# Moving the written-block and position passes, and the unseen-position mask, behind the first quarter of layer 1

## The chip, the cores and the metric

The kernel runs on one core of one Trainium2 chip. The metric is device time in microseconds (us), the median over several executions; lower is better. The core has engines that each work through their own queue in order: TensorE (PE, matrix products), VectorE (DVE), ScalarE (ACT), GpSimd (POOL), and SyncE (SP), which here only issues DMAs. They meet through semaphores: an instruction that waits holds up everything behind it in its own queue.

## The reference, cut to what matters

Two layers over 1024 tokens (32 sequences of 32, width 256), all in fp32. Layer 0: a gathered 32x32 mix per sequence, a LayerNorm attention, a LoRA feed-forward and a gated feed-forward. Layer 1: a causal attention (`L1_cond`), a linear attention over memory banks (`L1_attn`), a paged attention (`L1_cond2`), and a mixture of 16 experts (`L1_ffn`). The part that the change touches prepares the paged attention:

```python
pos = kv_lens[:, None] + jnp.arange(Tx)          # 32 new positions of each sequence
q, k = _rope(q, pos), _rope(k, pos)              # cos and sin of pos
blk = jnp.take_along_axis(block_tables, pos // BLOCK, axis=1)
k_blocks = k_blocks.at[blk, :, pos % BLOCK, :].set(k.transpose(0, 2, 1, 3))
v_blocks = v_blocks.at[blk, :, pos % BLOCK, :].set(v.transpose(0, 2, 1, 3))
k_all, v_all = (c[block_tables] for c in (k_blocks, v_blocks))
# attention over the last WINDOW = 128 keys at or before each position
```

Sequences may share blocks, so a key that a sequence reads can have been written by another one. The kernel therefore works out, for every slot of every block that is read, which new token wrote it last, or none. That is the search for the written blocks. Its result is a row number for every key, kept in `at`.

## The kernel before, in words

The 1024 tokens are worked in four quarters (`NQ = 4`) of 256. Layer 0's attention runs for quarters 0 to 3 (`mha`, L346, called in the loop at L464); `feed_forward(0)` (L558) follows; then come the preparations of the paged attention; then, in the loop at L903, `layer1(q)` and `feed_forward(q + 1)` for q = 0 to 3. The paged attention and the experts come last.

The order on each engine is not written out. The tile scheduler plays the program through with its own costs and, each time an engine comes free, takes of the instructions that are ready the one that was emitted first. So a part that is emitted later fills the gaps of the parts before it, and `feed_forward(q + 1)` fills those of `layer1(q)` on TensorE. `behind(first, *later)` (L178) adds an edge of order alone: on their engine, `later` come after `first`. `attended` is the last addition of layer 0's attention (L483); `weighted` is the list of the last softmax passes of each `mha` half (L403).

The steps that matter here, in their order of emission before the change:

- **The block rows** (L561 to L587, in pool `ix`): four rounds. POOL gathers the key and value blocks into `raw` (two tiles, tags a0 and a1 of `apool`), copies them into row order `rr` (two buffers), and SP stores each `rr` to `rows_d`.
- **The written blocks and the positions' rows** (L595 to L682): passes over `sw`, `fs`, `wb`, `eq`, then four rounds of `t`, `ok`, `most`, `last` (L610 to L633), and four of `ec`, `mt` (L647, L648) with `ovl`, all on DVE. SP stores `last` to `win_d`; POOL gathers `wsel` from it (L654), makes `newi`; SP stores it to `at_d`; POOL gathers `run` (L678) and casts it to `runf` (L682).
- **The rotation tables** (L685 to L718): `pos`, `ang`, `kf`, `r` on DVE, two Sin activations on ACT (L711), and eight products into `turn`.
- **The mask of unseen positions** (L727 to L744): pool `bad` loads a constant, POOL makes `low` and `bad` for 32 sequences, and fills `none`, which SP spreads over the experts' table `xs_d`. The profile shows its first POOL pass waiting for the last store of `rr`.
- **`layer1(q)`** (L765): `mha` makes scores from `QT` (L767), `KT`, `vblk` (L369) and `kb` (L378); then come the memory banks (L810 to L841), `x3T` (L845), and rotated keys and queries (L876). `x3T` and `qall` take the tags a0 and a1, thus the places of `raw`. In quarter 1, TensorE transposes `runf` into `at` (L849, L851). `at` is first read by the gathers of the paged attention (L945), and `bad` by its scores (L987).

## Time and profile before

| what | value |
|---|---|
| time, median of 3 runs | 712.08 us (706.6 to 713.12) |
| the profiled execution | 711.48 us |
| its span, first to last instruction | 709.2 us |
| mean granted TensorE clock | 0.914 of full speed |
| PE, DVE, ACT, POOL busy in the span | 83%, 53%, 26%, 27% |

The profiled execution lasts 711.48 us, of which 2.3 us lie outside the span. Its time is 0.6 us under the median. Times within the span are counted from its first instruction. In timeline rows the columns are the start, the duration, the engine, the line of the program, the operation, what it writes and reads, and how many such instructions were merged; in brackets stands how long the engine was idle before it and what ended that. Passes of one engine overlap by some 0.07 us, so that a row's duration is a little longer than the step to the next row.

### The profile page before, as it was taken

To read this page: it belongs to the slowest core of one execution; us is meant where nothing else is said; L and a number is where in the kernel's file an instruction comes from. 1 tells how busy PE (TensorE), PEld (TensorE's weight loads), DVE (VectorE), ACT (ScalarE), POOL (GpSimd) and SP (SyncE) were. 2 spreads that over 40 slices of the span, in tenths; PEclk is the share of its full clock that TensorE was granted. 3 is DMA by queue.
4 is the path that set the end of the run, shared out by engine and by line. 5 is a ranking of instruction groups with operands and counts; after the bars stand their busy time and mean duration, and the time that the engine had idled before them with its cause. 6 is when DMAs were issued, how large, how long until landed. Compare 5 with 4: busy or idle time off the path is not lost.

```text
span 709.2 us, 9084 instructions
## 1 busy us (share of the span) xinstructions
PE 585.9 (83%) x3246; PEld 452.0 (64%) x3246; DVE 377.3 (53%) x872; ACT 187.5 (26%) x492; POOL 192.2 (27%) x280
## 2 busy tenths in 40 slices
PE   3679999995999999999999986655888998079990
PEld 2457877872888867888678864443666665056660
DVE  4748476799544284423754244332577737035553
ACT  1313232322212031311313221022566623012220
POOL 4013003345569700000000000007664101724450
PEclk9959999997999999999999995685899999679996
DMA  6945003454363000000000063003221000224315
GB/s 167 380 154 66 18 1 121 132 150 108 100 201 96 0 1 1 16 0 1 1 1 15 1 257 142 1 26 105 85 71 49 1 1 15 104 66 125 115 48 178
DMA packets 37452, 55.35 MB, mean 78 GB/s; under 512 B 8906, under 2 KB 29536, under 8 KB 36576
## 3 DMA queue, kind: packets, MB, share of 16 engines
q1 hardware_dynamic: 27549, 37.62, 16.3%
q0 software_dynamic: 5904, 15.40, 8.1%
q10 hardware_dynamic: 3955, 1.75, 0.9%
q8 instruction: 26, 0.43, 0.3%
q14 instruction: 18, 0.15, 0.1%
HBM read 38.56 MB, written 18.17 MB: 80 GB/s over the span
## 4 chain that ended last, share of the span: by engine, by line
PE 59%; DVE 16%; issue 8%; POOL 7%; DMA 4%; ACT 4%; POOLq 0%; SPq 0%; DVEq 0%; ACTq 0%
PE ff L188 27%; PE mm L188 13%; POOL ys_d L1271 4%; DVE kb L378 3%; PE tr L412 3%; PE mm L835 3%; DVE vblk L369 2%; PE po L1011 2%; ACT sm L993 2%; PE tr L406 1%; PE sc L979 1%; PE sc L385 1%; POOL xs_d L1201 1%; DVE sm L987 1%; PE mm L1196 1%
## 5 line engine op out<-in xcount | busy, mean ns | idle before, releaser
L945 POOL DMA_INDIRECT kv<-rows_d,at x40 | 38.8, 970 | 245.2 <-DMA sh_g<-in_L_ffn_sWg 234.7
L583 POOL COPY rr<-raw 88x256 f32<-88x256 f32 x64 | 29.3, 489 | 89.0 <-PE tr L459 47.4
L524 DVE SCALAR_TENSOR_TENSOR th<-th,ff 128x512 f32<-128x512 f32 x32 | 21.7, 679 | 51.0 <-ACT th L523 50.9
L378 DVE TENSOR_TENSOR kb<-KT,con 128x1024 f32<-128x1024 f32 x32 | 38.3, 1218 | 9.2 <-ACT KT L473 5.6
L1271 POOL DMA_INDIRECT ys_d<-yb,xb x31 | 30.5, 985 | 44.9 <-DVE yb L1269 44.6
L385 PE MATMUL sc<-kb,QT 128*32 128x256 f32 x256 | 22.4, 424 | 20.1 <-DVE kb L378 15.8
L1256 PE MATMUL gu<-ew,xT 128*128 x124 | 34.4, 400 | 3.2 <-issue 2.5
L523 ACT ACTIVATE th<-ff 128x512 f32<-128x512 f32 x32 | 19.1, 597 | 64.8 <-PE ff L188 56.1
L188 PE MATMUL ff<-x,w_g 128*128 128x256 f32 x128 | 35.5, 392 | 0.0
L188 PE MATMUL ff<-x,w_u 128*128 128x256 f32 x128 | 34.3, 381 | 0.0
L188 PE MATMUL ff<-y,f_w_gate 128*128 128x256 f32 x128 | 31.5, 381 | 0.0
L188 PE MATMUL ff<-y,f_w_up 128*128 128x256 f32 x128 | 31.0, 380 | 0.0
L1250 PE MATMUL xt<-ident,xb 128*128 128x128 f32 x62 | 11.8, 291 | 21.7 <-DMA xb<-xs_d 21.6
L188 PE MATMUL ff<-h,d_Wd 128*128 128x256 f32 x128 | 29.8, 381 | 0.0
L188 PE MATMUL ff<-h,f_w_down 128*128 128x256 f32 x128 | 28.3, 379 | 0.0
L1256 PEld LDWEIGHTS gu<-ew,xT 128*128 128x128 f32 x124 | 23.1, 199 | 7.7 <-issue 2.8
L993 ACT ACTIVATE sm<-sm,mx 128x160 f32<-128x160 f32 x64 | 26.7, 418 | 4.6 <-DVE mx L991 3.6
L525 DVE SCALAR_TENSOR_TENSOR h<-th,ff 128x512 f32<-128x512 f32 x32 | 21.9, 684 | 10.7 <-PE ff L188 10.1
L188 PEld LDWEIGHTS ff<-x,w_g 128*128 128x128 f32 x128 | 23.9, 194 | 4.7 <-issue 1.6
L188 PEld LDWEIGHTS ff<-x,w_u 128*128 128x128 f32 x128 | 24.1, 190 | 4.0 <-issue 0.8
L979 PE MATMUL sc<-KT,qz 128*128 128x160 f32 x128 | 25.3, 335 | 1.7 <-DVE qz L965 1.3
L385 PEld LDWEIGHTS sc<-kb,QT 128*32 128x32 f32 x256 | 5.3, 111 | 33.3 <-DVE kb L378 22.4
(337 smaller groups left out, 1342.1 us busy)
## 6 DMA issues: line engine op xcount, KB each, us to landing
ew<-in_L_ffn_W SPq DMA_DIRECT2D x1, 6144.0 KB
rows_d<-rr SPq DMA_DIRECT2D x32, 176.0 KB
xs_d<-none SPq DMA_DIRECT2D x1, 3999.0 KB
xb<-xs_d SPq DMA_DIRECT2D x31, 129.0 KB
x<-in_x SPq DMA_DIRECT2D x4, 256.0 KB
w_u<-in_L_cond_Wu SPq DMA_DIRECT2D x1, 1024.0 KB
w_g<-in_L_cond_Wg SPq DMA_DIRECT2D x1, 1024.0 KB
d_Wd<-in_L_cond_Wd SPq DMA_DIRECT2D x1, 1024.0 KB
```

Source lines behind the costliest of these rows:

```text
L188: mm_ = te.matmul(ps, lhsT=a, rhs=b, start=j == 0, stop=j == len(pairs) - 1)
L378: v.tensor_tensor(kb, KT[:, m, js].rearrange("p (b k) -> p b k", b=4).unsqueeze(2).broadcast_to([P, 4, 8, 32]), m8.unsqueeze(1).unsqueeze( ...
L385: te.matmul(ps[32 * b4 : 32 * b4 + 32, m * 256 : (m + 1) * 256], lhsT=QT[:, m, j * P + 32 * b4 : j * P + 32 * b4 + 32], rhs=kb[:, b4].rear ...
L412: te.matmul(av[64 * (hg % 2) : 64 * (hg % 2) + 64, hg // 2, 32 * b4 : 32 * b4 + 32], lhsT=vblk[:, j, b4, hg, :], rhs=PT[:, hg, 32 * b4 : 3 ...
L524: v.scalar_tensor_tensor(flat(t), flat(t), 1.0, flat(pg), ALU.add, ALU.mult)
L525: v.scalar_tensor_tensor(flat(h[:, f : f + 2]), flat(t), 0.5, flat(pu), ALU.mult, ALU.mult)
L583: g_.tensor_copy(r[:, :, j].rearrange("p o g d -> p g o d"), raw[j].rearrange("p (g a o d) -> a p g o d", g=4, a=8, d=32)[a],)
L945: got = g_.indirect_dma_start(out=kv[:, a, :], out_offset=None, in_=rows_d, in_offset=bass.IndirectOffsetOnAxis(ap=at[:, g, a : a + 1], ax ...
L979: te.matmul(ps[:, h, :], lhsT=q.qz[:, b, h].rearrange("p g t -> p (g t)"), rhs=q.KT[:, b, :], start=True, stop=True,)
L993: s.activation(sm[:, h], sm[:, h], AF.Exp, bias=mx[:, h : h + 1], accum_out=q.su[:, b, h : h + 1])
L1256: te.matmul(pg[:, :D], lhsT=xT[:, k * P : (k + 1) * P], rhs=w[:, k * D : (k + 1) * D], start=k == 0, stop=k == 1)
L1271: g_.indirect_dma_start(out=ys_d, out_offset=bass.IndirectOffsetOnAxis(ap=xb[:, D + 1 :].bitcast(I32), axis=0), in_=yb, in_offset=None, bo ...
```

## The change

The preparations are cut into three. What stays where it was, ahead of `layer1(0)`: the block rows, and, moved up before the rest, the rotation tables. The written blocks and positions' rows become a function, `positions(after)`, and the mask and the table fill become `unseen()`. Both are called in the loop after `layer1(0)` and ahead of `feed_forward(1)`; the first passes of `positions` are ordered behind the last softmax pass of `layer1(0)` rather than behind `attended`. The pool `ix` is held open until then. No instruction is added or removed.

```diff
-        with tc.tile_pool(name="ix", bufs=1) as cp:
+        ix = ExitStack()
+        cp = ix.enter_context(tc.tile_pool(name="ix", bufs=1))
...
         bwf = cp.tile([NW, 1], F32, name="bwf")
         bcf = cp.tile([CP, NC4], F32, name="bcf")
         behind(attended, v.tensor_copy(bwf, blkw), v.tensor_copy(bcf, blkc))
...
+        pos = cp.tile([P, NG], F32, name="pos")
+        behind(attended, v.tensor_scalar(pos, kvt, C("p32"), None, ALU.add))
...
+            s.activation(cs[:, j].rearrange("p g i -> p (g i)"), r, AF.Sin)
...
+        def positions(after):
...
-            sw = slot(kvr, 0, "sw", cp, attended)
-            first_ = slot(kvb, WINDOW - 1, "fs", cp, attended)
+            sw = slot(kvr, 0, "sw", cp, after)
+            first_ = slot(kvb, WINDOW - 1, "fs", cp, after)
...
-            behind(attended, v.tensor_scalar(eq, bwr[:NW], bwf, None, ALU.is_equal))
+            behind(after, v.tensor_scalar(eq, bwr[:NW], bwf, None, ALU.is_equal))
...
             g_.tensor_copy(runf, run)
+            return runf
...
+        def unseen():
...
+            bp = ctx.enter_context(tc.tile_pool(name="bad", bufs=1, side="right"))
+            load_consts(bp, 4)
...
+            return bad, xs_d, ys_d
...
         for q in range(NQ):
             layer1(q)
+            if q == 0:
+                runf = positions(weighted[-1])
+                ix.close()
+                bad, xs_d, ys_d = unseen()
             if q + 1 < NQ:
                 x2T.append(feed_forward(q + 1))
```

More of the change, by code (lines that the diff above doesn't have):

```diff
@@ L558, in tile_layers @@
         x2T = [feed_forward(0)]
-        with tc.tile_pool(name="ix", bufs=1) as cp:
-            ovl = cp.tile([CP, NC4], I32, name="ovl")
-            load_consts(cp, 1)
-            bw_d = dram.tile([NW, 1], I32, name="bw_d")
-            nc.sync.dma_start(bw_d, blkw)
-            bwr = cp.tile([P, NW], I32, name="bwr")
-            nc.sync.dma_start(bwr, bw_d.rearrange("a b -> (a b)").partition_broadcast(P))
-            for c in range(NC4):
-                raw = [apool.tile([CP, ROW], F32, tag=f"a{j}", name=f"raw{j}") for j in range(2)]
-                for j, k in enumerate("kv"):
-                    g_.indirect_dma_start(
-                        out=raw[j],
-                        out_offset=None,
-                        in_=i[f"L1_cond2_{k}_blocks"],
-                        in_offset=bass.IndirectOffsetOnAxis(ap=blkc[:, c : c + 1], axis=0),
-                    )
-                dst = rows_d[c * CP * BLK : (c + 1) * CP * BLK, :].rearrange("(p a o) d -> a p o d", a=8, o=BLK // 8)
-                for a in range(8):
-                    r = cp.tile([CP, BLK // 8, 2, 4, 32], F32, tag="rr", name="rr", bufs=2)
-                    for j in range(2):
-                        g_.tensor_copy(
-                            r[:, :, j].rearrange("p o g d -> p g o d"),
-                            raw[j].rearrange("p (g a o d) -> a p g o d", g=4, a=8, d=32)[a],
-                        )
-                    nc.sync.dma_start(dst[a], r.rearrange("p o j g d -> p o (j g d)"))
-            bwf = cp.tile([NW, 1], F32, name="bwf")
-            bcf = cp.tile([CP, NC4], F32, name="bcf")
-            behind(attended, v.tensor_copy(bwf, blkw), v.tensor_copy(bcf, blkc))
-            sw = slot(kvr, 0, "sw", cp, attended)
-            first_ = slot(kvb, WINDOW - 1, "fs", cp, attended)
@@ new lines, in tile_layers @@
+        ix = ExitStack()
+        cp = ix.enter_context(tc.tile_pool(name="ix", bufs=1))
+        ovl = cp.tile([CP, NC4], I32, name="ovl")
+        load_consts(cp, 1)
+        bw_d = dram.tile([NW, 1], I32, name="bw_d")
+        nc.sync.dma_start(bw_d, blkw)
+        bwr = cp.tile([P, NW], I32, name="bwr")
+        nc.sync.dma_start(bwr, bw_d.rearrange("a b -> (a b)").partition_broadcast(P))
+        for c in range(NC4):
+            raw = [apool.tile([CP, ROW], F32, tag=f"a{j}", name=f"raw{j}") for j in range(2)]
+            for j, k in enumerate("kv"):
+                g_.indirect_dma_start(
+                    out=raw[j],
+                    out_offset=None,
+                    in_=i[f"L1_cond2_{k}_blocks"],
+                    in_offset=bass.IndirectOffsetOnAxis(ap=blkc[:, c : c + 1], axis=0),
+                )
+            dst = rows_d[c * CP * BLK : (c + 1) * CP * BLK, :].rearrange("(p a o) d -> a p o d", a=8, o=BLK // 8)
+            for a in range(8):
+                r = cp.tile([CP, BLK // 8, 2, 4, 32], F32, tag="rr", name="rr", bufs=2)
+                for j in range(2):
+                    g_.tensor_copy(
+                        r[:, :, j].rearrange("p o g d -> p g o d"),
+                        raw[j].rearrange("p (g a o d) -> a p g o d", g=4, a=8, d=32)[a],
+                    )
+                nc.sync.dma_start(dst[a], r.rearrange("p o j g d -> p o (j g d)"))
@@ new lines, in tile_layers @@
+        bwf = cp.tile([NW, 1], F32, name="bwf")
+        bcf = cp.tile([CP, NC4], F32, name="bcf")
+        behind(attended, v.tensor_copy(bwf, blkw), v.tensor_copy(bcf, blkc))
+        pos = cp.tile([P, NG], F32, name="pos")
+        behind(attended, v.tensor_scalar(pos, kvt, C("p32"), None, ALU.add))
+        ang = cp.tile([P, NG, 16], F32, name="ang")
+        v.tensor_tensor(
+            ang,
+            pos.unsqueeze(2).broadcast_to([P, NG, 16]),
+            C("inv").unsqueeze(1).broadcast_to([P, NG, 16]),
+            ALU.mult,
+        )
@@ new lines, in tile_layers @@
+        c1 = 6.28125
+        c2 = float(np.float32(np.round((2 * math.pi - c1) * 2.0**21) / 2.0**21))
+        c3 = 2 * math.pi - c1 - c2
+        angf = ang.rearrange("p g i -> p (g i)")
+        cs = cp.tile([P, 2, NG, 16], F32, name="cs")
+        for j, quarter in enumerate((0.25, 0.0)):
+            kf = cp.tile([P, NG * 16], F32, tag="kf", name="kf")
+            v.tensor_scalar(kf, angf, 1.0 / (2 * math.pi), quarter, ALU.mult, ALU.add)
+            v.tensor_scalar(kf, kf, 12582912.0, None, ALU.add)
+            v.tensor_scalar(kf, kf, 12582912.0, None, ALU.subtract)
+            r = cp.tile([P, NG * 16], F32, tag="r_", name="r_")
+            v.scalar_tensor_tensor(r, kf, -c1, angf, ALU.mult, ALU.add)
+            v.scalar_tensor_tensor(r, kf, -c2, r, ALU.mult, ALU.add)
+            v.scalar_tensor_tensor(r, kf, -c3, r, ALU.mult, ALU.add)
+            if quarter:
+                v.tensor_scalar(r, r, math.pi / 2, None, ALU.add)
+            v.tensor_scalar(r, r, 3.1415925, -3.1415925, ALU.min, ALU.max)
+            s.activation(cs[:, j].rearrange("p g i -> p (g i)"), r, AF.Sin)
@@ new lines, in tile_layers @@
+        for j, k in enumerate("qk"):
+            sc_ = cp.tile([P, 32], F32, name=f"scale{j}")
+            nc.sync.dma_start(sc_, i[f"L1_cond2_{k}_norm_scale"].partition_broadcast(P))
+            behind(attended, v.tensor_scalar(sc_, sc_, 1.0, (1.0 / 16.0, 1.0)[j], ALU.add, ALU.mult))
+            for f in range(2):
+                for a in range(2):
+                    v.tensor_tensor(
+                        turn[j][:, f, :, 16 * a : 16 * a + 16],
+                        cs[:, f],
+                        sc_[:, 16 * a : 16 * a + 16].unsqueeze(1).broadcast_to([P, NG, 16]),
+                        ALU.mult,
+                    )
@@ L682, in tile_layers @@
             g_.tensor_copy(runf, run)
-            pos = cp.tile([P, NG], F32, name="pos")
-            behind(attended, v.tensor_scalar(pos, kvt, C("p32"), None, ALU.add))
-            ang = cp.tile([P, NG, 16], F32, name="ang")
-            v.tensor_tensor(
-                ang,
-                pos.unsqueeze(2).broadcast_to([P, NG, 16]),
-                C("inv").unsqueeze(1).broadcast_to([P, NG, 16]),
-                ALU.mult,
-            )
-            c1 = 6.28125
-            c2 = float(np.float32(np.round((2 * math.pi - c1) * 2.0**21) / 2.0**21))
@@ L695, in tile_layers @@
-            c3 = 2 * math.pi - c1 - c2
-            angf = ang.rearrange("p g i -> p (g i)")
-            cs = cp.tile([P, 2, NG, 16], F32, name="cs")
-            for j, quarter in enumerate((0.25, 0.0)):
-                kf = cp.tile([P, NG * 16], F32, tag="kf", name="kf")
-                v.tensor_scalar(kf, angf, 1.0 / (2 * math.pi), quarter, ALU.mult, ALU.add)
-                v.tensor_scalar(kf, kf, 12582912.0, None, ALU.add)
-                v.tensor_scalar(kf, kf, 12582912.0, None, ALU.subtract)
-                r = cp.tile([P, NG * 16], F32, tag="r_", name="r_")
-                v.scalar_tensor_tensor(r, kf, -c1, angf, ALU.mult, ALU.add)
-                v.scalar_tensor_tensor(r, kf, -c2, r, ALU.mult, ALU.add)
-                v.scalar_tensor_tensor(r, kf, -c3, r, ALU.mult, ALU.add)
-                if quarter:
-                    v.tensor_scalar(r, r, math.pi / 2, None, ALU.add)
-                v.tensor_scalar(r, r, 3.1415925, -3.1415925, ALU.min, ALU.max)
-                s.activation(cs[:, j].rearrange("p g i -> p (g i)"), r, AF.Sin)
@@ L712, in tile_layers @@
-            for j, k in enumerate("qk"):
-                sc_ = cp.tile([P, 32], F32, name=f"scale{j}")
-                nc.sync.dma_start(sc_, i[f"L1_cond2_{k}_norm_scale"].partition_broadcast(P))
-                behind(attended, v.tensor_scalar(sc_, sc_, 1.0, (1.0 / 16.0, 1.0)[j], ALU.add, ALU.mult))
-                for f in range(2):
-                    for a in range(2):
-                        v.tensor_tensor(
-                            turn[j][:, f, :, 16 * a : 16 * a + 16],
-                            cs[:, f],
-                            sc_[:, 16 * a : 16 * a + 16].unsqueeze(1).broadcast_to([P, NG, 16]),
-                            ALU.mult,
-                        )
@@ L727, in tile_layers @@
-        bp = ctx.enter_context(tc.tile_pool(name="bad", bufs=1, side="right"))
-        load_consts(bp, 4)
-        bad = bp.tile([P, B, NPOS], mybir.dt.bfloat16, name="bad")
-        front = bp.tile([P, B], F32, name="front")
-        g_.tensor_scalar(front, kvr, -1.0, float(WINDOW - 1), ALU.mult, ALU.add)
-        for b in range(0, B, 2):
-            low = bp.tile([P, 2, NPOS], F32, tag="low", name="low")
-            for j in range(2):
-                g_.tensor_scalar(low[:, j, :], C("jp"), front[:, b + j : b + j + 1], None, ALU.is_lt)
-            g_.tensor_tensor(bad[:, b : b + 2, :], low, C("far").unsqueeze(1).broadcast_to([P, 2, NPOS]), ALU.add)
@@ L739, in tile_layers @@
-        xs_d = dram.tile([NB * P, XROW], F32, name="xs_d")
-        ys_d = dram.tile([2 * NT, D], F32, name="ys_d")
-        none = bp.tile([P, XROW], F32, name="none")
-        g_.memset(none, 0.0)
-        g_.memset(none[:, D + 1 :].bitcast(I32), int(SKIP))
-        nc.sync.dma_start(
-            xs_d.rearrange("(b p) d -> p b d", p=P), none.unsqueeze(1).broadcast_to([P, NB, XROW])
-        )
+            return runf
+        def unseen():
+            bp = ctx.enter_context(tc.tile_pool(name="bad", bufs=1, side="right"))
+            load_consts(bp, 4)
+            bad = bp.tile([P, B, NPOS], mybir.dt.bfloat16, name="bad")
+            front = bp.tile([P, B], F32, name="front")
+            g_.tensor_scalar(front, kvr, -1.0, float(WINDOW - 1), ALU.mult, ALU.add)
+            for b in range(0, B, 2):
+                low = bp.tile([P, 2, NPOS], F32, tag="low", name="low")
+                for j in range(2):
+                    g_.tensor_scalar(low[:, j, :], C("jp"), front[:, b + j : b + j + 1], None, ALU.is_lt)
+                g_.tensor_tensor(bad[:, b : b + 2, :], low, C("far").unsqueeze(1).broadcast_to([P, 2, NPOS]), ALU.add)
+            xs_d = dram.tile([NB * P, XROW], F32, name="xs_d")
+            ys_d = dram.tile([2 * NT, D], F32, name="ys_d")
+            none = bp.tile([P, XROW], F32, name="none")
+            g_.memset(none, 0.0)
+            g_.memset(none[:, D + 1 :].bitcast(I32), int(SKIP))
+            nc.sync.dma_start(
+                xs_d.rearrange("(b p) d -> p b d", p=P), none.unsqueeze(1).broadcast_to([P, NB, XROW])
+            )
+            return bad, xs_d, ys_d
```

## The prediction

> **What bounds the kernel now.** I read the page first: TensorE (PE) is busy 83% of the span and heads the chain that ended last. So I looked for places where PE stands still, with the waits of PE and then its rows in order of time. Between layer 0 and the second quarter of layer 1 there are two, both behind the passes that the change moves:

> ```profile
> 152.08 1.56 PE L188 MATMUL mm<-res,wb_q 128*128 128x256 f32 x6 [1.55 <-DVE res L555]
> ...
> 159.17 1.03 PE L188 MATMUL ff<-x,w_u 128*128 128x256 f32 x4
> 168.75 2.22 PE L385 MATMUL sc<-kb,QT 128*32 128x256 f32 x16 [8.56 <-DVE kb L378]
> ```

> PE waits 1.55 us for x2 (`res`) and 8.56 us for the keys `kb` of the first scores. DVE at that time:

> ```profile
> 137.68 0.17 DVE L273 TENSOR_SCALAR sw<-kvr 128x32 int32<-128x32 int32 x1
> ...
> 161.71 0.16 DVE L631 TENSOR_TENSOR last<-last,most 96x16 f32<-96x16 f32 x1
> ...
> 161.96 0.67 DVE L767 TENSOR_TENSOR QT<-mm,beta 128x512 f32<-128x512 f32 x1
> 162.56 2.36 DVE L718 TENSOR_TENSOR turn<-cs,scale 128x128 f32<-128x128 f32 x8
> 164.95 2.51 DVE L369 COPY vblk<-V 32x128 f32<-32x128 f32 x8
> 167.47 2.36 DVE L378 TENSOR_TENSOR kb<-KT,con 128x1024 f32<-128x1024 f32 x2
> ```

> From 137.68 to 161.96 DVE has no gap, and QT, whose product PE ended at about 153.6, starts only at 161.96. What it costs is read by setting the first quarter beside the third, which has no preparation beside it. I cut both at the same events (first query product, first score, end of the interleaved part, next quarter's product):

> ```profile
> core 0: us, PE busy (x) PEld busy (x) DVE busy (x) ACT busy (x) POOL busy (x), PEclk, DMA share, GB/s
> ...
> 149.50:168.75 19.25, 9.15 (x41) 7.25 (x39) 19.11 (x60) 6.72 (x14) 6.50 (x14) 0.86 0.52 135
> 168.75:213.40 44.65, 44.59 (x269) 33.90 (x270) 25.10 (x44) 9.09 (x18) 27.58 (x47) 0.95 0.51 145
> 213.40:245.60 32.20, 32.20 (x151) 28.35 (x150) 12.82 (x26) 5.79 (x11) 28.97 (x38) 1.00 0.16 46
> ...
> 331.00:336.70 5.70, 5.70 (x31) 4.74 (x29) 2.57 (x4) 0.93 (x2) 0.00 (x0) 1.00 0.00 0
> 336.70:380.70 44.00, 42.26 (x268) 32.82 (x268) 23.37 (x41) 10.90 (x24) 0.00 (x0) 1.00 0.00 1
> 380.70:416.10 35.40, 35.40 (x166) 31.09 (x165) 13.12 (x27) 8.97 (x14) 0.00 (x0) 1.00 0.09 30
> ```

> The first quarter takes 19.25 + 44.65 + 32.20 = 96.1 us, the third 5.70 + 44.00 + 35.40 = 85.1. The **ceiling** of the gain is the difference, 11.0 us. It is roughly the 10.1 us of standing PE, and the clock of 0.95 after it (0.05 x 44.65 = 2.2 us), less 1.7 us that the third quarter's PE also waits.

> **The moved passes and where they land.** From 137.5 to 161.96 DVE spends 24.5 us. Of these feed_forward(0) takes 3.0 (two `th`, two `h`, two `res`, by the steps between rows), `bwf`, `bcf` and the end of x1 0.2, the rotation tables up to `r` 3.1. The rest, **18.1 us**, is what `positions` takes along. After the change it waits for the last softmax pass of quarter 0 (182.3 in the old trace). The stretch from there to the end of the quarter's interleaved part:

> ```profile
> 182.30:213.40 31.10, 31.10 (x197) 25.24 (x196) 12.64 (x26) 6.16 (x13) 20.34 (x39) 1.00 0.51 149
> ```

> DVE is busy 12.64 of 31.10 us, so 18.5 are free for 18.1: room, but no more than that. PE has no gap at all there. Its rows for layer 1's own chain in this stretch add up to 18.8 us; the other 12.3 are feed_forward(1), which fills the waits. `positions` is emitted ahead of feed_forward(1), so the scheduler prefers its passes to the `th` and `h` that free PE's sums. Two things soften this. The old order shows what a later-emitted group gets: from 150 on, `kf` and `r` alternate with `t` and `ok` one for one, because each pass waits for the one before it in its own chain; only while `ec`, `mt` ran beside `t`, `ok` (139 to 148) was a third group shut out. And only four feed_forward passes (h, th, h, th) lie there; the `h` at 184.8 can wait until PE's next need of that bank at 195.5. Bounds: 0, and full starvation (a rival below). Each of some 14 passes on layer 1's chain can also stand half a moved pass (0.25 us) longer, 3.5 us that the filler mostly covers. I take **1.5 us**, nearer to nothing because filler is there.

> **x3T behind POOL.** x3T takes the place of `raw`, so L845 also waits for POOL's last `rr` copy:

> ```profile
> 198.96 0.73 POOL L583 COPY rr<-raw 88x256 f32<-88x256 f32 x2
> ```

> The quarter's x3T comes 45.3 us after its first product in quarter 1 (290.92 - 245.63), so after the change at 149.5 + 45.3 = 194.8 at the earliest, where POOL now ends at 199.7. But 6 us of POOL's last round (from 181.06) are the gathers of `positions`, which now come later; the two rounds before took 14.4 and 15.6 us, so the last should end near 196. A wait of 0 to 1.5 us, beside the same 1.5 us of DVE delay: not added again. Behind L845 on DVE stand feed_forward's last `h` and the rotations.

> **Rotation tables and Sin.** These 27 passes (3.1 us, then 2.4 for `turn`) stay ahead of layer 1 and now run from 137.7, in time that `sw` to `ok` held; PE is busy there until 150.5. The two Sin fall between the Tanh of feed_forward(0) at 137.67 and 141.12. The row: one table load is

> ```profile
> 162.14 1.28 ACT L523 ACT_TABLE_LOAD   x1
> ```

> Load, Sin (0.31) and reload put the second Tanh some 1.8 us late; its `h` ends at 145.8 instead of 144.0; PE first needs it at 142.6 + 6 x 0.43 = 145.2. Loss 0.6 if Sin goes ahead, 0 if not: I take **0.3**. [...] In this trace Sin at 157.09 starts 1.29 us after its load, so I count by the row.

> **The mask under the next quarter.** The POOL chain from `last` to `runf` took from 167.55 to 199.0; it now starts near 202 and ends near 221 (store and landing 2.5, four gathers 5.5 and landing 2.6, five passes 1.6, store 2.5, gather and cast 3.7). PE reads `runf` at 291.24 before, near 280 after: 59 us to spare. The mask then takes 202.17 to 244.6, 42 us, so it runs from about 224 to 266, and `bad` is first read after 485. But the second quarter's attention, near 240, now has POOL beside it. The row: eight `vblk` copies took 2.51 us with POOL copying (above) and

> ```profile
> 252.29 1.84 DVE L369 COPY vblk<-V 32x128 f32<-32x128 f32 x8
> ```

> with POOL idle, while passes with PSUM or two inputs (0.69 us) took the same in both. [...] the trace has `kb` at 2.36 for two in both quarters. So **0.6 us** for quarter 1 and, as its POOL copies remain beside it, **0.6** for quarter 0 against my model.

> **DMAs moved.** `win_d`, `at_d` (two), the mask's constant and the 4 MB fill of `xs_d` go to SP later. Behind them stands the store of quarter 0's new rows (217.79 before); its tile is written again near 240, so up to 20 us of delay cost nothing, and more would hold ACT there. The fill is needed at 598.9. POOL's queue has nothing else to give until 479.31.

> **The sum.** 11.0 - 1.5 - 0.3 - 0.6 - 0.6 = 8.0 us. On the profiled execution's 711.48 us (span 709.2 and 2.3 around it) that is **703.5 us**. The median shown is 712.08, 0.6 above that execution, inside the spread of the three runs.

> **Rivals.**
> 1. *Everything is hidden* (15%): no delay on DVE, no POOL effect: 711.48 - 11.0 = 700.5. For it: filler on PE. Against: 18.1 us into 18.5.
> 2. *Part of the filler is lost* (18%): feed_forward(1) is shut out for part of the stretch. The last quarter shows a layer 1 with no filler: from its last softmax pass (433.6) to the last product of rotated rows (472.2) 38 us instead of 31, with clock 0.75. No filler at all would cost 38 + 12.3 - 31.1 = 19.2 us. A quarter of that, 4.8, gives 711.48 - 8.0 + 3.3 (4.8 in place of 1.5) = 706.8.
> 3. *Slower* (6%): full starvation, all DVE slots going to `positions` until its end: 711.48 - 9.5 + 19.2 = 721.2. It decides from half the filler lost: then 9.6 us eat the 9.5. Against: the one-for-one alternation seen.
> 4. *The change does not free QT* (6%): `turn` is queued ahead of QT and waits for a late Sin, as it waited until 162.1 before. Sin should be out by 147 and QT is wanted near 152; a slip to 155 leaves 5 us, 706.5.

> The forecast itself has 55%, with a range of its own of 701.5 to 705.5.

> **How the numbers follow.** About 1% (7.1 us) is what a measurement of this kernel can tell from no change; the three runs lie 6.5 us apart. Faster by over 1% is below 705.0: rival 1 and some 85% of the forecast, 62%. Slower is rival 3, 5%. The rest, 33%, is within 1%. The range goes from 699.0 (rival 1 and some scatter) to 709.0 (rivals 2 and 4 and scatter).

> **What the profile after would show.** Right: QT within 1 us of its product near 152.5, first score near 156, no PE wait over 2 us there; first quarter 86 to 89 us; `sw` to `last` between about 170 and 205, mixed with `th` and `h`; L845 near 196; mask until about 266; second quarter's `vblk` at 2.3 to 2.5 us. Wrong: PE waiting for `th`, `h` or ff banks between 170 and 203, L845 waiting for POOL for over 2 us, QT behind `turn`, or a wait for `runf` near 280.

## The result, and the profile after

The changed kernel takes 705.22 us (median of 20 runs, 698.98 to 707.41), the one before 712.17 us in as many runs beside it (706.6 to 717.5). The ratio is 0.9897 with a 95% interval of 0.9873 to 0.9921: faster by 1.0%, 1.7 us behind the forecast of 703.5 us and within its range. The profiled execution took 705.67 us, with a span of 703.9 us at a mean clock of 0.91.

I cut the spans at the starts of the first query product of each quarter (`mm<-res,wb_q`):

| | start of quarter 0 | quarter 0 | quarter 1 | quarter 2 | quarter 3 to `wqkv` | the rest |
|---|---|---|---|---|---|---|
| before | 149.50 | 96.13 | 85.34 | 84.99 | 52.54 | 240.70 |
| after | 150.03 | 87.73 | 88.76 | 84.99 | 54.69 | 237.70 |
| difference | +0.53 | -8.40 | +3.42 | 0.00 | +2.15 | -3.00 |

The sum is -5.3 us, the difference of the spans. So the change brought 8.4 us in the quarter that it was made for, and 3.4 us were given back in the next one. The last two columns nearly cancel; they are taken up at the end.

TensorE at the scores of quarter 0, in order of time:

```profile
155.73 0.64 PE L385 MATMUL sc<-kb,QT 128*32 128x256 f32 x8
...
160.98 0.64 PE L385 MATMUL sc<-kb,QT 128*32 128x256 f32 x8 [0.62 <-DVE kb L378]
162.61 0.64 PE L385 MATMUL sc<-kb,QT 128*32 128x256 f32 x8 [1.00 <-DVE kb L378]
164.02 0.87 PE L188 MATMUL ff<-z,bl_g 128*128 128x256 f32 x2 [0.76 <-DVE z L507]
```

The waits of 1.55 and 8.56 us are gone. What is left is 2.38 us in three pieces, where the same places in the undisturbed quarter 2 have 1.74 us (0.18, 1.00 and 0.56). DVE in that quarter:

```profile
152.39 0.69 DVE L772 TENSOR_TENSOR QT<-mm,beta 128x512 f32<-128x512 f32 x1 [1.73 <-PE mm L188]
154.30 2.36 DVE L378 TENSOR_TENSOR kb<-KT,con 128x1024 f32<-128x1024 f32 x2 [1.22 <-ACT KT L353]
156.69 2.06 DVE L369 COPY vblk<-V 32x128 f32<-32x128 f32 x8
...
172.81 0.16 DVE L273 TENSOR_SCALAR sw<-kvr 128x32 int32<-128x32 int32 x1
...
199.70 0.17 DVE L676 TENSOR_TENSOR last<-last,most 96x16 f32<-96x16 f32 x1
199.78 0.69 DVE L850 TENSOR_TENSOR x3T<-mm,res 128x512 f32<-128x512 f32 x1
```

QT goes as soon as its product is out, and the search (`sw` to `last`) runs from 172.8 to 199.9. The rows by stretch, cut as before at first query product, first score, end of the interleaved part and next quarter, for quarters 0 and 1:

```profile
core 0: us, PE busy (x) PEld busy (x) DVE busy (x) ACT busy (x) POOL busy (x), PEclk, DMA share, GB/s
150.00:155.70 5.70, 5.70 (x27) 4.75 (x26) 2.52 (x4) 0.88 (x2) 0.88 (x1) 1.00 0.86 179
155.70:206.00 50.30, 47.92 (x286) 37.29 (x286) 42.93 (x96) 14.20 (x30) 20.50 (x37) 0.97 0.35 97
206.00:237.80 31.80, 31.80 (x149) 27.90 (x149) 11.33 (x24) 4.72 (x8) 22.97 (x35) 1.00 0.49 144
237.80:243.80 6.00, 5.73 (x27) 4.71 (x25) 2.89 (x4) 1.21 (x3) 5.54 (x8) 1.00 0.00 1
243.80:291.00 47.20, 44.06 (x275) 34.07 (x276) 25.60 (x43) 10.36 (x23) 17.60 (x18) 0.96 0.00 1
```

In the second stretch DVE is busy for 42.93 of 50.30 us, and PE stands for 2.38 us, just the three waits above: the search took no filler from PE. In the last row PE stands for 3.14 us. There the scores read:

```profile
243.84 0.64 PE L385 MATMUL sc<-kb,QT 128*32 128x256 f32 x8 [0.31 <-DVE kb L378]
...
249.92 0.64 PE L385 MATMUL sc<-kb,QT 128*32 128x256 f32 x8 [1.46 <-DVE kb L378]
251.64 0.64 PE L385 MATMUL sc<-kb,QT 128*32 128x256 f32 x8 [1.08 <-DVE kb L378]
252.84 0.94 PE L188 MATMUL ff<-z,bl_g 128*128 128x256 f32 x2 [0.56 <-DVE z L507]
```

The waits add up to 3.41 us, 1.67 more than in quarter 2. What made `kb` late is on DVE, with POOL's mask beside it (the second row is the first pass of the first row alone):

```profile
242.03 2.89 DVE L378 TENSOR_TENSOR kb<-KT,con 128x1024 f32<-128x1024 f32 x2 [1.22 <-ACT KT L353]
242.03 1.76 DVE L378 TENSOR_TENSOR kb<-KT,con 128x1024 f32<-128x1024 f32 x1 [1.22 <-ACT KT L353]
244.95 2.97 DVE L369 COPY vblk<-V 32x128 f32<-32x128 f32 x8
...
248.56 1.22 DVE L378 TENSOR_TENSOR kb<-KT,con 128x1024 f32<-128x1024 f32 x1
...
250.29 1.30 DVE L378 TENSOR_TENSOR kb<-KT,con 128x1024 f32<-128x1024 f32 x1
```

```profile
240.43 1.34 POOL L741 TENSOR_SCALAR low<-con,front 128x160 f32<-128x160 f32 x2
241.85 0.86 POOL L742 TENSOR_TENSOR bad<-low,con 128x320 bf16<-128x320 f32 x1
242.80 3.24 POOL L741 TENSOR_SCALAR low<-con,front 128x160 f32<-128x160 f32 x2
...
248.59 1.92 POOL L742 TENSOR_TENSOR bad<-low,con 128x320 bf16<-128x320 f32 x1
```

The two first `kb` passes took 2.89 us instead of 2.36, the eight `vblk` copies 2.97 instead of 1.84, together 1.66 us more, and two `low` passes of POOL 3.24 instead of 1.34. Not every pass paid. Of the four `kb` passes one took 1.76 us, and that is the one that began at 242.03, while `bad` (241.85 to 242.71) was running; the others kept 1.21 to 1.30. The `bad` that began 0.03 us after the `kb` of 248.56 took 1.92 us instead of 0.86. So in these rows the pass that starts second is the one that is stretched.

Then PE's clock fell, as the stretch with the waits and the one after it show (columns as above, clock third from the end):

```profile
249.75:253.16 3.41, 1.59 (x17) 0.64 (x18) 3.41 (x6) 0.63 (x1) 3.31 (x3) 1.00 0.02 5
253.16:256.57 3.41, 3.41 (x10) 2.69 (x9) 2.74 (x6) 0.19 (x1) 3.15 (x5) 0.50 0.00 0
```

Half the clock for 3.41 us costs 1.7 us (0.5 x 3.41). Waits of 1.67 and clock of 1.7 make the 3.4 us of quarter 1.

### The profile page after: what moved, and what is told of

Same layout as the page of the kernel before. It is cut to its first block, busy times and chain, and to the rows that moved or that the text cites. A ratio compares the mean times of both kernels' runs of the same rounds, so it can differ in the third digit from the quotient of the medians.

```text
span 703.9 us, 9084 instructions
## 1 busy us (share of the span) xinstructions
PE 588.1 (84%) x3246; PEld 453.6 (64%) x3246; DVE 377.3 (54%) x872; ACT 187.4 (27%) x492; POOL 196.1 (28%) x280
## 4 chain that ended last, share of the span: by engine, by line
PE 62%; DVE 13%; issue 8%; POOL 6%; ACT 5%; DMA 4%; POOLq 0%; ACTq 0%; DVEq 0%; SPq 0%
PE ff L188 29%; PE mm L188 14%; POOL ys_d L1280 4%; DVE kb L378 4%; PE tr L412 3%; PE mm L840 3%; PE po L1020 2%; DVE vblk L369 2%; ACT sm L1002 2%; PE tr L406 1%; DVE sm L996 1%; POOL xs_d L1210 1%; PE sc L988 1%; PE sc L385 1%; PE mm L1205 1%
## 5 line engine op out<-in xcount | busy, mean ns | idle before, releaser
L378 DVE TENSOR_TENSOR kb<-KT,con 128x1024 f32<-128x1024 f32 x32 | 39.2, 1245 | 10.8 <-ACT KT L473 5.9
L188 PE MATMUL ff<-x,w_g 128*128 128x256 f32 x128 | 36.7, 401 | 0.0
L188 PE MATMUL ff<-x,w_u 128*128 128x256 f32 x128 | 34.1, 381 | 0.0
L385 PE MATMUL sc<-kb,QT 128*32 128x256 f32 x256 | 22.2, 421 | 14.1 <-DVE kb L378 10.1
L523 ACT ACTIVATE th<-ff 128x512 f32<-128x512 f32 x32 | 19.1, 597 | 52.0 <-PE ff L188 42.4
L188 PE MATMUL ff<-y,f_w_gate 128*128 128x256 f32 x128 | 31.5, 381 | 0.0
L188 PE MATMUL ff<-y,f_w_up 128*128 128x256 f32 x128 | 31.0, 380 | 0.0
L188 PE MATMUL ff<-h,d_Wd 128*128 128x256 f32 x128 | 29.8, 381 | 0.0
L188 PE MATMUL ff<-h,f_w_down 128*128 128x256 f32 x128 | 28.3, 379 | 0.0
L188 PEld LDWEIGHTS ff<-x,w_g 128*128 128x128 f32 x128 | 24.4, 198 | 5.0 <-issue 2.0
L188 PEld LDWEIGHTS ff<-x,w_u 128*128 128x128 f32 x128 | 24.2, 191 | 4.1 <-issue 0.8
L741 POOL TENSOR_SCALAR low<-con,front 128x160 f32<-128x160 f32 x32 | 25.8, 816 | 3.0 <-DMA con<-in_const 1.5
L188 PEld LDWEIGHTS ff<-y,f_w_gate 128*128 128x128 f32 x128 | 24.0, 190 | 4.0 <-issue 0.8
L188 PEld LDWEIGHTS ff<-h,d_Wd 128*128 128x128 f32 x128 | 24.0, 190 | 3.9 <-issue 0.8
```

The costliest lines, as they stand in the source:

```text
L188: mm_ = te.matmul(ps, lhsT=a, rhs=b, start=j == 0, stop=j == len(pairs) - 1)
L378: v.tensor_tensor(kb, KT[:, m, js].rearrange("p (b k) -> p b k", b=4).unsqueeze(2).broadcast_to([P, 4, 8, 32]), m8.unsqueeze(1).unsqueeze( ...
L385: te.matmul(ps[32 * b4 : 32 * b4 + 32, m * 256 : (m + 1) * 256], lhsT=QT[:, m, j * P + 32 * b4 : j * P + 32 * b4 + 32], rhs=kb[:, b4].rear ...
L741: g_.tensor_scalar(low[:, j, :], C("jp"), front[:, b + j : b + j + 1], None, ALU.is_lt)
```

## The experiments

Ratios are to the kernel before, measured beside each version on the same chip. Chips and executions differ in the last stages (the kernel before took 711.83 and, later, 721.34 us on one chip and 721.18 on another; over the twelve profiles the rest of the kernel took 237.3 to 251.6), so the lengths of quarters 0 and 1 are the sharper measure; quarter 2 took 84.98 or 84.99 us in every profile.

**The mask after quarter 1's softmax.**

```diff
-        def unseen():
+        def unseen(after):
...
-            g_.tensor_scalar(front, kvr, -1.0, float(WINDOW - 1), ALU.mult, ALU.add)
+            fr = g_.tensor_scalar(front, kvr, -1.0, float(WINDOW - 1), ALU.mult, ALU.add)
+            tc.add_manual_dep(fr.ins, after.ins.name, waits, reason="beside no softmax")
...
-                bad, xs_d, ys_d = unseen()
+            if q == 1:
+                bad, xs_d, ys_d = unseen(weighted[-1])
```

> The changed kernel, with the mask of unseen positions made to wait on POOL for the last softmax pass of quarter 1, so that it runs in the second half of that quarter and no longer beside its attention. Theory (the mask on POOL slows the DVE passes of quarter 1's attention, and TensorE's clock falls after the waits): eight vblk copies back from 2.97 us to 1.84, quarter 1 back from 88.8 us to about 85.4, first quarter unchanged at 87.7; ratio to the kernel before about 0.985, some 702 us. Rival A (the clock falls there by itself, or another moved part does it): quarter 1 stays near 88.8, ratio 0.990. Rival B (the mask costs the same wherever it runs): the 3.4 us turn up between 257 and 300.

Measured: 0.9836 (0.9806 to 0.9866); quarters 87.68 and 85.34 us. The passes of quarter 1 in this kernel:

```profile
241.29 2.36 DVE L378 TENSOR_TENSOR kb<-KT,con 128x1024 f32<-128x1024 f32 x2 [1.22 <-ACT KT L353]
243.68 1.84 DVE L369 COPY vblk<-V 32x128 f32<-32x128 f32 x8
```

They are back at their old durations, and all of the 3.4 us came back. This version beats the kernel before. Its interval also lies below that of the changed kernel (0.9873 to 0.9921), though the two were not run side by side.

**The mask's move alone.** From the kernel before; the searches stay ahead of layer 1, `unseen` is called after `layer1(0)` and its first pass waits for the last rotated query of quarter 0.

```diff
+            if q == 0:
+                bad, xs_d, ys_d = unseen(turned[-1])
```

> The kernel before, with nothing moved but the mask: it waits for the last rotated query of quarter 0 and so runs beside quarter 1's attention; the searches stay where they were. Theory: first quarter stays at 96.1 us, quarter 1 goes from 85.3 to about 88.8; ratio about 1.005. Rival A (not the mask): quarter 1 stays at 85.3, ratio 1.000.

Measured: 1.0037 (1.0018 to 1.0056), quarters 97.40 and 89.07 us. `kb` takes 3.19 us and `vblk` 3.06; quarter 1 loses 3.7 us, as in the full change. This half of the change has a price and no gain. Of the 1.3 us in quarter 0, 0.7 stand in the waits of PE (a new one of 1.55 us for `AV` at 188.77, and 1.10 less for the keys); what brought them, and the rest, is not traced.

**The search rounds done twice**, emitted where the change has them (rounds 0 to 3, and again into the same tiles).

```diff
-            for c in range(4):
+            for n, c in enumerate((0, 1, 2, 3) * 2):
...
-                if c:
+                if n:
```

> The changed kernel, with the four search rounds (t, ok, most, last) made twice, some 13.7 us more of passes on VectorE behind the first quarter's softmax; the second time repeats the first. Theory (VectorE has room there and the passes alternate with those of feed_forward(1), so that TensorE keeps its filler): first quarter grows by 0 to 1 us from 87.7; ratio about 0.990 to 0.992. Rival C (feed_forward(1) is starved of VectorE, and the forecast's 1.5 us were the beginning of it): first quarter grows by 3 us or more, ratio 0.994 or above.

Measured: 0.9979 (0.9959 to 0.9999), quarters 93.68 and 86.89 us. PE now does wait for feed_forward(1):

```profile
212.15 1.90 PE L188 MATMUL ff<-h,d_Ad 128*128 128x256 f32 x4 [4.07 <-DVE h L525]
```

So starvation, my rival on the slower side, exists: it sets in when about twice the work is emitted ahead of the filler. Quarter 1 has the mask beside it as in the change, and the same waits of PE (1.46, 1.08 and 0.56 us), but here the clock stayed at 1.00, also after these rows:

```profile
249.92:253.34 3.42, 1.84 (x14) 0.91 (x12) 3.36 (x7) 0.00 (x0) 3.24 (x4) 1.00 0.52 131
253.34:256.75 3.41, 1.89 (x14) 1.28 (x15) 3.41 (x6) 0.63 (x1) 3.33 (x3) 1.00 0.02 5
```

It cost 86.89 - 85.34 = 1.55 us, of which the waits are 1.36. So of the 3.4 us one half came in all three profiles with the mask beside these scores (the changed kernel, the mask's move alone, and this one; a fourth, further below, has its matmuls in another order), the other in two of them. What decides on it can be read from the rows: here the waits are split over two stretches of 3.41 us, 1.58 and 1.52, while the changed kernel had 1.82 in one. The last section says why the stretches are cut so.

**No mask.** Leaves out the mask's passes (`bad` is filled with zeros).

```diff
-            for b in range(0, B, 2):
+            g_.memset(bad, 0.0)
+            for b in range(0, 0, 2):
```

> The changed kernel, with the mask's 48 passes on POOL left out and its tile set to zero by one pass, so that the paged attention sees all its positions. Theory: quarter 1 at 85.4 us, time as in the run with the mask after quarter 1's softmax, ratio about 0.985. Rival A: quarter 1 stays near 88.8, ratio 0.990.

Measured: 0.9838 (0.9806 to 0.987), quarters 87.45 and 85.35 us. The same as with the mask moved on; so the mask beside quarter 1 is what costs, and later it is free. In quarter 0 the clock did not fall here, and yet the quarter is no shorter: PE waits 1.23 us for `AV` (174.99) instead, behind the softmax on DVE. So in this profile the work on DVE took what the clock left.

**The edge of order taken back** (`positions` still emitted after `layer1(0)`; the mask as in the first experiment).

```diff
-                runf = positions(weighted[-1])
+                runf = positions(attended)
```

> The run with the mask after quarter 1's softmax, with one edge changed: the passes of the search are ordered behind the end of layer 0's attention again, while they are still emitted after layer 1's first quarter. Theory (what frees QT is the place of emission, since the scheduler takes first what was emitted first; the edge alone does little): the passes spread over DVE's gaps from 139 us on, first quarter within 1 us of 87.7. Rival D (the edge is what does it: passes let in between 139 and 170 hold up QT, vblk and kb, each by what is left of a pass): first quarter 89 us or more.

Measured: 1.0012 (0.9987 to 1.0036), quarter 0 at 98.94 us. I had thought that the place of emission frees QT. It does: QT starts at 152.10. But the search passes fill DVE, and z of feed_forward(1), emitted behind them, is not done by 172, so that PE has nothing to fill its waits with:

```profile
168.87 1.12 PE L406 MATMUL tr<-ident,sm 128*128 128x128 f32 x4 [6.27 <-DVE sm L403]
```

```profile
160.70:206.00 45.30, 36.88 (x215) 29.13 (x216) 28.99 (x61) 9.18 (x18) 22.48 (x39) 0.85 0.34 90
```

PE stands for 8.4 us in that stretch, at a clock of 0.85. All of the gain hangs on the edge, as long as the search is emitted ahead of feed_forward(1).

**The search emitted after feed_forward(1)** (mask as in the first experiment, edge as in the change).

```diff
-            if q == 0:
-                runf = positions(weighted[-1])
-                ix.close()
+            first = weighted[-1]
...
                 x2T.append(feed_forward(q + 1))
+            if q == 0:
+                runf = positions(first)
+                ix.close()
```

> The run with the mask after quarter 1's softmax, with the search emitted after feed_forward(1), so that the passes of feed_forward(1) go first on VectorE. Theory (with the search made once, VectorE had room, so who goes first makes no difference): first quarter 87.7 us give or take 0.5, ratio as without this, about 0.984. Rival C (the search costs feed_forward(1) something): first quarter 86.5 or less.

Measured: 0.9846 (0.9803 to 0.9889), quarters 88.19 and 85.35 us. No gain in quarter 0 over the change's order: with one search the filler lost nothing that could be given back.

**The double search emitted after feed_forward(1).** The edit of the double search and the last one together.

> The four search rounds made twice, emitted after feed_forward(1), with the mask after quarter 1's softmax. The search made twice and emitted ahead of feed_forward(1) took the first quarter to 93.7 us, with TensorE waiting 4.1 us for the last h of feed_forward(1). Theory (that h stood behind search passes and rotations because they were emitted first; it is the order and not the 13.7 us of work): first quarter 88.5 us or less. Rival (VectorE has not the time for the second search in this quarter, in whatever order): 91 us or more.

Measured: 0.9914 (0.9883 to 0.9945), quarters 87.57 and 85.36 us. With the same double work as before, quarter 0 is 6.1 us shorter (93.68). So the double work starves the filler only in the order that prefers it.

**PE's wait filled** with three matmuls into a spare PSUM tile between the two score halves of quarter 1 (the changed kernel otherwise).

```diff
+                if fill and j == 1:
+                    dm = tr.tile([P, 4, P], F32, tag="tr", name="dm")
+                    for n in range(fill):
+                        x = te.matmul(dm[:, :2].rearrange("p a n -> p (a n)"), lhsT=ident, rhs=w["q"][:, 0, :], start=True, stop=True)
+                        behind(shot, x)
```

> The changed kernel, with the mask still beside quarter 1's attention, and three more matmuls of TensorE (128x256, result not used, about 0.43 us each) between the two halves of the scores of quarter 1, so that TensorE waits about 1.3 us less there. Theory (of the 3.4 us that quarter 1 lost, half is the longer wait for kb and half the clock that falls after it): the granted clock after the scores stays near 1.0 instead of 0.66, quarter 1 at about 87.0 us instead of 88.8 although TensorE does more. Rival E (the clock falls for another reason than TensorE's wait): quarter 1 stays at 88.8 or above.

Measured: 0.9986 (0.9965 to 1.0006), quarter 1 at 91.20 us. It says nothing on its question: the spare tile shares two buffers with the transposed weights, so the added matmuls, and the scores behind them, went only at 256.19, and PE stood 4.37 us in one piece before that.

**The keys' pass done twice, with POOL idle.** From the first experiment; the first `kb` pass of quarter 1's second half is repeated into the same tile. PE's order up to the transposes is the same.

```diff
+                    for n in range(2 if again and (j, m) == (1, 0) else 1):
-                    v.tensor_tensor(
+                        v.tensor_tensor(
...
-            AV = mha(x2T[q], wa1, q_out, s.copy, s.copy)
+            AV = mha(x2T[q], wa1, q_out, s.copy, s.copy, again=q == 1)
```

> The version with the mask after quarter 1, whose quarter 1 took 85.34 us with waits of TensorE of 0.18, 1.00 and 0.56 us at the scores and no loss of clock. Here the first kb pass of quarter 1's second half is done twice into the same tile, 1.18 us more on VectorE, with GpSimd idle. The wait for it should grow from 0.18 to some 1.4 us, the three together to some 2.9, about what the mask beside the quarter made of them (3.4). Theory (the clock falls because of the waits): granted clock of some 0.7 for about 5 us after them, quarter 1 at 85.3 + 1.2 + 1.5 = 88.0 us. Rival (it was GpSimd's work beside TensorE that lowered the clock): clock 1.0 throughout and quarter 1 at 86.5.

Measured: 0.9883 (0.983 to 0.9935), quarter 1 at 88.84 us, 3.5 more than without the repeat.

```profile
247.50 0.64 PE L386 MATMUL sc<-kb,QT 128*32 128x256 f32 x8 [1.91 <-DVE kb L379]
249.14 0.64 PE L386 MATMUL sc<-kb,QT 128*32 128x256 f32 x8 [1.01 <-DVE kb L379]
250.34 1.22 PE L188 MATMUL ff<-z,bl_g 128*128 128x256 f32 x2 [0.56 <-DVE z L508]
```

```profile
246.64:250.05 3.41, 1.28 (x16) 0.34 (x16) 3.41 (x5) 0.63 (x1) 0.00 (x0) 1.00 0.02 5
250.05:253.46 3.41, 3.12 (x7) 2.53 (x8) 2.82 (x6) 0.00 (x0) 0.00 (x0) 0.50 0.00 0
```

POOL (the fifth engine of a row) has 0.00 here and until 257, and the clock falls all the same, to half for 3.41 us, which is 1.7 us again. So GpSimd's work was not needed for the fall (and in the double search it was there without one): here 2.13 us of waits in one stretch of 3.41 (3.41 - 1.28) came before the fall with POOL idle. DVE's 1.2 us more cost 1.7 in waits and 1.7 in clock.

**Edge taken back, with the search emitted after feed_forward(1).**

```diff
-                runf = positions(first)
+                runf = positions(attended)
```

> The version with the search emitted after feed_forward(1), whose first quarter took 88.2 us, but with the edge of the search back at the attention scores of layer 0's last quarter, so that the search may start at once. Theory (with the edge moved back and the search emitted first, quarter 0 took 98.9 us because the search shut out z and so starved TensorE of filler; the order of emission decides, the edge as such does not): first quarter about 88 to 89 us, z of feed_forward(1) on VectorE ahead of the search's later passes, no wait of TensorE over 2 us. Rival (the edge is needed wherever the search is emitted): first quarter of 91 us or more, with QT or the first kb pass late behind search passes.

Measured: 0.9894 (0.9833 to 0.9955); quarter 0 at 86.33 us, the shortest of all, quarter 1 at 85.35.

```profile
153.43 0.67 DVE L773 TENSOR_TENSOR QT<-mm,beta 128x512 f32<-128x512 f32 x1
...
155.35 2.34 DVE L378 TENSOR_TENSOR kb<-KT,con 128x1024 f32<-128x1024 f32 x2
...
163.49 0.67 DVE L507 TENSOR_TENSOR z<-ff,amask 128x512 f32<-128x512 f32 x1
```

z goes at 163.49, among search passes, and PE has its filler: no wait is over 1 us. The edge is needed only because the search is emitted ahead of feed_forward(1). Against the same order with the edge (88.19) quarter 0 is 1.9 us shorter, but 1.7 of that is a fall of the clock which that profile has and this one lacks. The run without the mask lacks it too and took 87.45, so a search that may start early, in DVE's room before 150, may be worth some 1.1 us; one profile does not show it. Over the whole kernel the interval is too wide to set this version above the two at 0.984.

## Why the prediction was right, and where not

**The ceiling and quarter 0: right.** Forecast 96.1 - 11.0 + 1.5 + 0.3 + 0.6 = 87.5 us, measured 87.73. QT, the first score (156 forecast, 155.73) and the search (170 to 205 forecast, 172.8 to 199.9) came where they were put.

**DVE's congestion (1.5): the sum holds, its contents only in part.** No `th` or `h` was late, and PE had no idle time between 164 and 237. The 2.7 us over quarter 2 are 0.6 more at the scores, half the clock for 3.41 us from 164.41 (1.7), and 0.4 that quarter 1 had over quarter 2 before the change too (85.34 against 84.99). So the sum came out in part by luck: 1.7 of it is a fall of the clock, which the forecast did not have. Without the mask, at full clock, PE met the DVE queue later and lost 1.4 of this; with the search emitted last and no edge, also at full clock, it did not. How much of the 1.5 was DVE's is thus not settled.

**What moved (18.1): too large.** `ec`, `mt` and `ovl`, some 2 us, have no edge and stayed ahead of layer 1 (139.56 to 145.2).

**x3T behind POOL: no wait,** as taken. POOL's last four `rr` copies began at 192.07 and took 1.80 us, so they ended at 193.9, where I had 196; L850 ran at 199.78, set by DVE.

**Sin: 0 instead of 0.3.** The load went behind the second Tanh, so nothing was late. The forecast priced a load between the two Tanh; here from load to Sin it was 1.30 us (1.29 in the kernel before), and each of this profile's 17 table loads took 1.28 us.

```profile
141.65 0.60 ACT L523 ACTIVATE th<-ff 128x512 f32<-128x512 f32 x1 [2.86 <-DVE r__1325 L616]
143.58 1.28 ACT L622 ACT_TABLE_LOAD   x1 [1.34 <-DVE r__1325 L621]
144.88 0.31 ACT L622 ACTIVATE cs<-r__1325 128x128 f32<-128x128 f32 x1
```

**The mask under the next quarter (0.6): the term that was mis-sized, 3.4 measured.** Place and time were right (218.96 to 262.4; forecast 224 to 266), and so was the kind of cost. Three things were missed. First, I took the `vblk` row beside block-row copies (2.51 us) for the mask's case; beside the mask it took 2.97. Secondly, I counted no delay of `kb`, because it had 2.36 us in both quarters before. Measured, the first two `kb` passes grew by 0.53 us beside the mask. The old trace could have told what a pass of POOL beside `kb` costs, on POOL's side:

```profile
165.62 1.53 POOL L583 COPY rr<-raw 88x256 f32<-88x256 f32 x4 [1.65 <-DMA rows_d<-rr]
168.81 3.36 POOL L583 COPY rr<-raw 88x256 f32<-88x256 f32 x4 [1.66 <-DMA rows_d<-rr]
```

The second row began inside a `kb` pass (the row of 167.47 to 169.83) and has another beside it; its copies took 3.36 us instead of 1.53, and the `kb` passes, which had started first, lost nothing. Thirdly, I counted DVE's delay and not what it does to PE's clock, which doubled it in this profile (though not in that of the double search). With 3.4 in place of 0.6 the forecast would have been 706.3 us. The profiled execution took 705.67. The median of 705.22 lies nearer to the 703.5 of the forecast than that, but the medians differ by 7.0 us and the spans of the two profiles by 5.3, so part of this nearness is chance.

**The rivals.** Everything hidden: not so. Filler lost: not with one search, but 6 us with two. QT not freed: not so. The slower side's mechanism is real; with one search the edge keeps it away.

**The late stages.** Quarter 3 took 2.15 us longer, with the same instructions and waits. Most of it, 1.79 us, is one product that still ran at half clock. First before, then after:

```profile
444.41 1.99 PE L188 MATMUL mm<-AV,wl_q 128*128 128x256 f32 x8 [0.68 <-ACT AV L803]
```

```profile
440.35 3.78 PE L188 MATMUL mm<-AV,wl_q 128*128 128x256 f32 x8 [0.67 <-ACT AV L808]
```

Over the ten experiments that stage took 51.8 us in three, 53.4 in one and 54.5 to 55.5 in six, in no relation to the edits. It follows the time at half clock within the stage: 27.3 to 30.7 us of it in the profiles of up to 53.4 us (the one before among them), 37.5 or 41.0 in the longer ones. What makes the difference is not shown. The 3.0 us on the other side I count as chance of the single profile: over all twelve, the rest of the kernel took 237.3 to 251.6 us.

## What to carry to other kernels

Work that is moved out of a full stretch must be priced in the stretch where it lands, by rows of the same pair of passes side by side, read on both engines, since here the one that started second was stretched (`kb` from 1.22 to 1.76 us, `bad` from 0.86 to 1.92). The wait that follows on TensorE must be priced with its clock: here 1.82 us of waits within 3.41 us were followed by 3.41 us at half clock, 1.7 us more. Where a scheduler prefers what is emitted first, emit the work that may wait behind the filler that feeds TensorE; an edge of order is needed only where that is not done. A pass of GpSimd that nobody needs for 200 us belongs beside a stretch in which TensorE does not wait for VectorE: behind quarter 1's softmax the mask left that quarter at 85.34 us here, beside it at 88.76.
